# Group-norm statistics moved from VectorE's bn_stats to ScalarE's accumulator passes in a Mamba-then-attention kernel

## The chip, the cores and the metric

The kernel runs on one core of one Trainium2 chip. The metric is the device time of one execution in microseconds; the kernel before took 8108.69 us (median of three runs, 8093.1 to 8114.99). The engines are named as the profile names them: PE is TensorE's matmul, PEld its weight load, DVE is VectorE, ACT is ScalarE, POOL is GpSimd, SP issues DMAs. L464 is line 464 of the kernel before.

## The reference

The input x is 4 × 512 × 64 × 64 in float32: 4 batches, 512 channels, 4096 positions. Two blocks follow one another, each on a group norm of its input:

```python
x = x + mamba_block(gn(x))        # layer 0
x = x + linear_attention(gn(x))   # layer 1

def gn(v, G=32, eps=1e-5):        # mean and variance over 16 channels and all positions
    g = v.reshape(B, G, C // G, H, W)
    m, s = mean(g, (2, 3, 4)), var(g, (2, 3, 4))
    return ((g - m) / sqrt(s + eps)).reshape(v.shape)
```

The Mamba block normalises the channels of every position, splits the 512 channels into four chunks of 128, and runs a state-space scan over the 4096 positions of each chunk (256 inner channels, 16 states each), gated by a silu. Its output is normalised again, projected and added to x; the sum is called x1 here. The attention block needs the mean and the variance of x1 over a whole batch before it can start, because its group norm goes over all positions. These statistics of x1 are what the change is about.

## The kernel before, in words

Positions are cut into tiles of 512 (NT = 8 a batch), so a tile of x or x1 is 128 partitions × 4 channel groups × 512 (NC = 4). A *step* is one chunk of one tile of one batch: 4 × 8 × 4 = 128 steps in that order, and a step has 16 *slots* (SLOTS). "Tile (1,2)" is tile 2 of batch 1. In a slot, `slot` (L618) issues for two groups of 32 inner channels with 4 states: two scans on VectorE (L632), whose decay factors dA come from an exponential on ScalarE into one of three PSUM buffers (`decay`, L606, issued three scans ahead), whose inputs bx come from POOL (`drive`, L614, issued two slots ahead), and a product of the states with C on VectorE (L655), whose other factor c_all PE puts into a single PSUM buffer. PE then folds the states into y. In slots 4 and 11 of a step two products stand behind each other, in 5 and 12 none.

Everything else is woven in by hand: at the end of each slot, `after` (L1006) runs what is due and takes pieces from generators in the queues `ahead` (the norm of the next tile), `late` (a finished tile leaving), `rest` (attention of the batch before) and `light` (statistics of the next batch's input). The program order on each engine is the order in which this Python issues. Engines work in order, so an instruction on ScalarE stands behind all that was issued before it. Two spots of a step load ScalarE most: in slot 3 two softplus between two activation table loads (L1025, L512, L1027), in slot 10 a silu over 2048 elements between two loads (L946, L1047); the decays of the next slot come behind them.

A queue's piece says with what it yields when it may go on: a bare `yield` waits for the credit that limits matmul work per slot, `yield "free"` doesn't.

A finished tile leaves through `projected` (L433), four slots after the accumulating DMA of L461 has added x to the projection. Before, four `bn_stats` on VectorE (L464) then take the tile's statistics in two pieces of two, each 128 × 512, the tile is stored to x1 in DRAM by SP, and its SBUF buffer (one of three, shared with attention and the input statistics) is released two slots later. This takes place in the step of the next tile's last chunk, in most cases in slots 2 and 3. Behind the last tile of a batch, `attention` starts; `stats_end` (L313) turns the 8 × 6 numbers of each channel into a mean and a variance (four `bn_aggr`, L317) and then into the group's scale and offset. The attention of the last batch has no loop beside it and runs alone at the end of the kernel, and so do the last tile's statistics.

Of the kernel before, what the change touches and what calls it, by code (L numbers as in the profile page):

```python
# [8 lines left out]
F32 = mybir.dt.float32  # L9
BF16 = mybir.dt.bfloat16  # L10
AF = mybir.ActivationFunctionType
ALU = mybir.AluOpType
AX = mybir.AxisListType

P = 128
T = 512
# [8 lines left out]
def kernel(  # L25
# [24 lines left out]
    nc = tc.nc  # L50
    B, C, L = x.shape
    NC = C // P
    NT = L // T
# [11 lines left out]
    small = ctx.enter_context(tc.tile_pool(name="small", bufs=2))  # L65
    wk = ctx.enter_context(tc.tile_pool(name="wk", bufs=2))
# [12 lines left out]
    def work_bank(name, behind=1):  # L79
        held[0] += behind  # L80
        return ps_w.tile([P, T], F32, tag="w", name=name)

    def free(n=1):
        held[0] -= n

    def later(n, what):

        done = []

        def both():  # L90
            what()
            done.append(True)

        if now[0] is None:
            both()
        else:
            due.append((now[0] + n, both))
        return done
# [5 lines left out]
    def until(*done):  # L104
        while not all(done):
            yield "wait"

    def pause(n):
        return until(later(n, lambda: None))

    def room(when="wait"):

        while now[0] is not None and held[0] >= limit[0]:
            yield when
# [3 lines left out]
    def cols(v, b):  # L118
        return v[b].rearrange("(c p) l -> p c l", p=P)

    def mm(out_, lhsT, rhs, abreast=1, **how):

        work["mm"] += (0.25 if rhs.dtype == BF16 else 1.0) * rhs.shape[-1] / T / abreast
        nc.tensor.matmul(out_, lhsT, rhs, **how)  # L124
# [9 lines left out]
    def no_tile(spare=0):  # L134
        return now[0] is not None and held_x[0] + spare >= TILES

    def new_tile(name):
        held_x[0] += 1
        return wk.tile([P, NC, T], F32, tag="x", name=name, bufs=TILES)
# [168 lines left out]


    def stats_tile(name):  # L310
        return small.tile([P, NC, NT, 6], F32, tag="stats", name=name)

    def stats_end(stats, name):  # L313

        mv = small.tile([P, NC, 2], F32, tag="mv", name=f"mv_{name}")
        for c in range(NC):
            nc.vector.bn_aggr(mv[:, c, :], stats[:, c, :, :].rearrange("p t s -> p (t s)"))  # L317
        cm = small.tile([P, NC], F32, tag="cm", name=f"cm_{name}")
        nc.vector.tensor_copy(cm, mv[:, :, 0])
        yield from room()  # L320
        pm = work_bank(f"pm_{name}")
        mm(pm[:, 0:NC], grp, cm, start=True, stop=True)
        gm = small.tile([P, NC], F32, tag="gm", name=f"gm_{name}")
        nc.vector.tensor_copy(gm, pm[:, 0:NC])
        dev = small.tile([P, NC], F32, tag="dev", name=f"dev_{name}")
        nc.vector.tensor_tensor(dev, cm, gm, ALU.subtract)
        nc.vector.tensor_tensor(dev, dev, dev, ALU.mult)
        nc.vector.tensor_tensor(dev, dev, mv[:, :, 1], ALU.add)
        pv = pm[:, NC : 2 * NC]
        mm(pv, grp, dev, start=True, stop=True)  # L330
        gr = small.tile([P, NC], F32, tag="gr", name=f"gr_{name}", bufs=4)
        nc.vector.tensor_scalar(gr, pv, 1e-5, None, ALU.add)
        free()
        nc.gpsimd.tensor_tensor(gr, gr, mhalf, ALU.pow)
        off = small.tile([P, NC], F32, tag="off", name=f"off_{name}", bufs=4)
        ngm = small.tile([P, NC], F32, tag="ngm", name=f"ngm_{name}", bufs=4)
        nc.vector.tensor_scalar(ngm, gm, -1.0, None, ALU.mult)
        nc.vector.tensor_tensor(off, ngm, gr, ALU.mult)
        return gr, off, ngm
# [93 lines left out]
    def projected(ym, stats, x1, b, t):  # L433

        nm = f"{b}_{t}"
        yield from layer_norm(ym, f"b_{nm}", False)
        while no_tile():
            yield "wait"
        xt = new_tile(f"xr_{nm}")
        taken = []  # L440

        def take(o, pp):
            nc.scalar.activation(xt[:, o, :], pp, AF.Identity, bias=pb[:, o : o + 1])
            free()

        for o in range(NC):
            yield from room()
            pp = work_bank(f"pp_{nm}_{o}")
            for c in range(NC):
                mm(  # L450
                    pp, w_pr[:, c, o * P : (o + 1) * P], ym[:, c, :],
                    start=(c == 0), stop=(c == NC - 1),
                )
                if c == 1:
                    yield "more"
            taken.append(later(1, lambda o=o, pp=pp: take(o, pp)))
            yield
        yield from until(*taken)
        yield from pause(1)

        nc.gpsimd.dma_start(xt, cols(x, b)[:, :, t * T : (t + 1) * T], accum_op=ALU.add)  # L461
        yield from pause(4)
        for o in range(NC):
            nc.vector.bn_stats(stats[:, o, t, :], xt[:, o, :])  # L464
            if o % 2:
                yield
        nc.sync.dma_start(x1, xt)
        later(2, free_x)


    def inputs(f, xn, c, nm):
# [220 lines left out]
    def stats0(stats, b):  # L692

        for t in range(NT):
            xt = yield from load_x(b, t, "s")
            yield
            for c in range(NC):
                nc.vector.bn_stats(stats[:, c, t, :], xt[:, c, :])
                if c == NC - 1:
                    later(1, free_x)  # L700
                if c % 2:
                    yield "wait" if c == NC - 1 else None

    def attention(b, x1s, stats):
# [49 lines left out]

        fetch(0, "a")
        yield
        norm = yield from stats_end(stats, f"b{b}")
        yield
        for v in range(NT * SUB):
            t, u = divmod(v, SUB)  # L760
# [62 lines left out]
        gr, _, ngm = norm  # L823
# [46 lines left out]
        for o in range(NC):  # L870
            for k in range(P // BLK):
                r = slice(k * BLK, (k + 1) * BLK)
                v = m3[r, o, o * P + k * BLK : o * P + (k + 1) * BLK]
# [35 lines left out]
    norms, stats1, x1s = {}, {}, {}  # L909
# [6 lines left out]
    def input_norm(b):  # L916
        stats = stats_tile(f"st0_{b}")
        yield from stats0(stats, b)
        norms[b] = yield from stats_end(stats, f"a{b}")
        yield  # L920

    def tile_norm(b, t):
# [5 lines left out]

    def leave(b, t):
        if t == 0:  # L930
            stats1[b] = stats_tile(f"st1_{b}")
            x1s[b] = [
                dram.tile([P, NC, T], F32, tag="x1", name=f"x1_{b}_{i}", bufs=3 * NT)
                for i in range(NT)
            ]
        ym = xn[b, t][:, :, NTAP - 1 : NTAP - 1 + T]
        yield from projected(ym, stats1[b], x1s[b][t], b, t)
        if t == NT - 1:
            add_to(rest, attention(b, x1s[b], stats1[b]))
# [10 lines left out]
    def add_to(queue, pieces):  # L950
        queue.append([pieces, None])
# [3 lines left out]
    def one(queue, may=ANYWHERE):  # L955
# [10 lines left out]
        return False  # L966

    run(input_norm(0))
    run(tile_norm(0, 0))
    run(step_inputs(0))  # L970
# [21 lines left out]
    with tc.manual_schedule():  # L992
        credit, seen, mix, held[0], held_x[0] = 0.0, work["mm"], iter(()), 0, 0
        for n, (b, t, c) in enumerate(steps):
            f, nm = fs[n], names[n]
# [6 lines left out]
            if c == 0 and t == 0 and b + 1 < B:  # L1002
                add_to(light, input_norm(b + 1))
            assert c != 2 or not ahead
            for s in range(SLOTS):
                def after():  # L1006
# [21 lines left out]
                    if s == 6 and before is not None:  # L1028
                        pb_, pt_, pc_ = steps[n - 1]
                        with_skip(before, xn[pb_, pt_], pc_)  # L1030
                        if pc_ == NC - 1:
                            add_to(late, leave(pb_, pt_))
# [46 lines left out]
    out_proj(fs[N - 1], xn[B - 1, NT - 1], NC - 1, names[N - 1])  # L1079
    with_skip(fs[N - 1], xn[B - 1, NT - 1], NC - 1)  # L1080
    add_to(late, leave(B - 1, NT - 1))
    while late or rest:
        one(late) or one(rest)
# [53 lines left out]
```

## Time and profile before

| | us |
|---|---|
| median of three runs | 8108.69 |
| the profiled execution, device time | 8103.21 |
| its span, first to last instruction | 8101.5 |
| DVE busy | 7158.1 (88%) |
| POOL busy | 6888.6 (85%) |
| PE busy | 6487.2 (80%) |
| ACT busy | 5365.5 (66%) |
| L464, bn_stats of x1 on DVE, 128 of them | 80.6, mean 671 ns |
| L606, decays on ACT, 4096 | 2787.8, mean 689 ns |

A row of the groups gives the line, engine, operation, output and inputs with their shape, then after the first bar the busy time and the mean of one in ns, after the second the engine's idle time just before these instructions and what ended it. A row of the waits gives who waited for whom, the sum in us, how often, and the longest. A row of the timeline gives start and duration in us, the engine, line and operation, how many followed one another, and in brackets the idle time ahead of it and what ended that.

### The profile page before, as it was taken

What the parts mean: (1) busy time and instruction counts of PE and PEld (TensorE: products, weight loads), DVE (VectorE), ACT (ScalarE), POOL (GpSimd) and SP (SyncE); (2) the same over time, 40 slices, a digit from 0 to 9 for tenths busy, and PEclk for the clock granted to TensorE, in tenths of its full rate; (3) what the DMA queues carried; (4) which work ended last, traced back from release to release, by engine and by line L of the source; (5) the groups of instructions that cost most, each with busy time, mean ns of one, the idle gap of its engine ahead of it and who ended that gap; (6) DMA issues with size and microseconds to landing.
All of it is one profiled execution on the core that took longest, in us unless ns stands there. A gap on an engine that the chain in (4) does not pass through costs nothing.

```text
span 8101.5 us, 92105 instructions
## 1 busy us (share of the span) xinstructions
PE 6487.2 (80%) x24800; PEld 2116.5 (26%) x24800; DVE 7158.1 (88%) x6891; ACT 5365.5 (66%) x7841; POOL 6888.6 (85%) x4597
## 2 busy tenths in 40 slices
PE   5677777667888888887788888888788888888699
PEld 1111112111222222322132222222122222322144
DVE  5999999999999999999999999999999999999700
ACT  4666677676677767676777767676777777766421
POOL 4999999999999988899989989898999989889600
PEclk8787878788899999998898999899799999999699
DMA  5666666666666666676756666677666666677402
GB/s 159 167 164 159 154 147 153 157 155 166 162 169 156 156 161 153 173 191 169 170 144 171 165 163 159 149 182 184 157 163 157 154 154 148 157 185 187 113 32 88
DMA packets 829195, 1265.95 MB, mean 156 GB/s; under 512 B 183912, under 2 KB 317560, under 8 KB 816384
## 3 DMA queue, kind: packets, MB, share of 16 engines
q1 hardware_dynamic: 804736, 1222.32, 60.1%
q0 software_dynamic: 16896, 33.56, 2.4%
q10 hardware_dynamic: 7040, 4.20, 0.2%
q8 instruction: 194, 3.18, 0.2%
q14 instruction: 329, 2.70, 0.1%
HBM read 1052.78 MB, written 206.57 MB: 155 GB/s over the span
## 4 chain that ended last, share of the span: by engine, by line
DVE 21%; PE 19%; DMA 19%; POOL 15%; issue 10%; SPq 9%; ACT 6%; POOLq 0%; DVEq 0%; ACTq 0%
DVE h L632 13%; POOL bx L614 11%; DMA d_all<-d_rows 11%; DVE h L655 6%; SPq L581 6%; PE pq L124 5%; DMA b_all<-b_rows 4%; SPq L531 3%; ACT dA L606 3%; PE pc L124 3%; PE pr L124 3%; PE y L124 2%; DMA c_sb<-c_rows 2%; POOL h L643 2%; POOL dt L520 1%
## 5 line engine op out<-in xcount | busy, mean ns | idle before, releaser
L614 POOL TENSOR_TENSOR bx<-d_all,b_all 128x1024 f32<-128x1024 f32 x2048 | 4815.8, 2370 | 51.4 <-DVE h L632 34.1
L632 DVE TENSOR_TENSOR_SCAN h<-dA,st,bx 128x512 f32<-128x512 f32 x3584 | 4425.2, 1268 | 59.0 <-ACT dA L606 49.5
L606 ACT ACTIVATE dA<-d_all,a_t 128x512 f32<-128x512 f32 x4096 | 2787.8, 689 | 1936.0 <-DVE h L632 1893.6
L655 DVE TENSOR_TENSOR h<-h,c_all 128x768 f32<-128x768 f32 x2048 | 1908.8, 932 | 301.9 <-PE c_all L124 293.5
L643 POOL TENSOR_TENSOR h<-h,c_sb 128x512 f32<-128x512 f32 x1024 | 1298.6, 1268 | 145.8 <-DMA c_sb<-c_rows 49.7
L124 PE MATMUL y<-h,fold 128*32 128x512 f32 x8192 | 1287.8, 705 | 140.7 <-POOL h L643 136.9
L124 PE MATMUL c_all<-parts,sel 128*128 128x384 bf16 x1024 | 369.8, 361 | 1112.7 <-DVE h L655 1110.5
L124 PE MATMUL pc<-xn,w_cv 128*128 128x512 f32 x2048 | 1068.2, 657 | 189.4 <-DVE xn L406 127.2
L124 PE MATMUL pq<-w_qk,xa 128*128 128x512 f32 x2048 | 989.8, 616 | 1.6 <-ACT xa L344 1.6
L632 DVE TENSOR_TENSOR_SCAN h<-dA,bx 128x512 f32<-128x512 f32 x512 | 601.6, 1207 | 60.3 <-ACT dA L606 55.9
L124 PEld LDWEIGHTS pc<-xn,w_cv 128*128 128x128 f32 x2048 | 394.1, 203 | 819.3 <-issue 455.9
L124 PEld LDWEIGHTS <-sel 128*128 128x128 bf16 x1280 | 127.5, 100 | 1792.5 <-DVE h L655 1552.8
L642 POOL COPY st<-h 128x4 f32<-128x4 f32 x1024 | 207.3, 202 | 436.4 <-DVE h L632 392.9
L124 PEld LDWEIGHTS pq<-w_qk,xa 128*128 128x128 f32 x2048 | 404.2, 200 | 455.6 <-issue 432.3
L124 PE MATMUL pr<-xb,m 128*128 128x512 f32 x1024 | 503.8, 630 | 7.3 <-DMA xb<-x 4.0
L124 PE MATMUL pp<-xn,w_pr 128*128 128x512 f32 x1024 | 487.5, 602 | 3.8 <-DVE xn L406 3.8
L124 PEld LDWEIGHTS y<-h,fold 128*32 128x32 f32 x8192 | 171.0, 115 | 719.2 <-issue 291.0
L124 PE MATMUL y<-xz,dg 32*32 32x512 f32 x2048 | 340.5, 741 | 0.0
L679 POOL TENSOR_TENSOR xz<-xz 128x512 f32<-128x512 f32 x256 | 325.0, 1270 | 2.7 <-ACT xz L676 2.7
L124 PE MATMUL pd<-xz,w_xp 128*128 128x512 f32 x512 | 317.3, 752 | 7.8 <-ACT xz L946 7.8
L520 POOL TENSOR_TENSOR dt<-dt,xz 128x1024 f32<-128x1024 f32 x128 | 302.1, 2360 | 22.1 <-DMA c_rows<-dt 20.9
L730 ACT ACTIVATE kq<-pq 128x512 f32<-128x512 f32 x256 | 150.9, 590 | 242.9 <-PE pq L124 240.0
(156 smaller groups left out, 5919.5 us busy)
## 6 DMA issues: line engine op xcount, KB each, us to landing
d_all<-d_rows SPq DMA_DIRECT2D x2048, 256.0 KB, 6.6
b_all<-b_rows SPq DMA_DIRECT2D x4096, 64.0 KB, 2.2
d_rows<-dt SPq DMA_DIRECT2D x256, 512.0 KB, 3.7
c_sb<-c_rows SPq DMA_DIRECT2D x4096, 16.0 KB, 1.8
xs<-in_x_dram SPq DMA_DIRECT2D x32, 1024.0 KB, 6.5
xn<-in_x_dram SPq DMA_DIRECT2D x32, 1024.0 KB, 5.8
xr<-in_x_dram POOLq DMA_DIRECT2D x32, 1024.0 KB, 10.6
x<-xr SPq DMA_DIRECT2D x32, 1024.0 KB, 6.6
```

The source lines that it names most:

```text
L124: nc.tensor.matmul(out_, lhsT, rhs, **how)
L520: nc.gpsimd.tensor_tensor(f["both"][:, 1], f["both"][:, 0], f["xz"][:, 0], ALU.mult)
L531: nc.sync.dma_start(d[k * BLK : (k + 1) * BLK, v], src)
L581: nc.sync.dma_start(dst[k * BLK : (k + 1) * BLK, :], rows_[q * KS + k, :].partition_broadcast(BLK))
L606: nc.scalar.activation(dAs[k], fs[n]["d_all", e][:, 0, j, :], AF.Exp, scale=a_t[:, e, j, q : q + 1])
L614: nc.gpsimd.tensor_tensor(bxs[g], fs[n]["d_all", e][:, 1, jj * 2 : jj * 2 + 2, :], bc(b_all[g // JJ], 2), ALU.mult)
L632: nc.vector.tensor_tensor_scan(h[:, j, :], dAs.pop(2 * g + i), bxs[g][:, i, :], 0.0 if t == 0 else st[:, c, e, q, j : j + 1], ALU.mult, AL ...
L642: nc.gpsimd.tensor_copy(st[:, c, e, q, :], h[:, :, T - 1])
L643: nc.gpsimd.tensor_tensor(h[:, :, CUT:], h[:, :, CUT:], bc(c_sb.pop(g // JJ), NJ), ALU.mult)
L655: nc.vector.tensor_tensor(own, own, bc(c_all[g // JJ], 2), ALU.mult)
L679: nc.gpsimd.tensor_tensor(f["xz"][:, 1, e, :], f["xz"][:, 1, e, :], f["xz"][:, 0, e, :], ALU.mult)
L730: nc.scalar.activation(qk[i], pq, AF.Relu)
```

## The change

For the first tile of a batch the four `bn_stats` stay; their result is aggregated at once, into a mean and a variance per channel. For the other seven tiles, ScalarE runs two passes over each of the four 128 × 512 parts of the tile: `Identity` with the negated mean of the first tile as its bias, and `Square` with the same bias. Each writes a throwaway output (in the buffers called "res") and has its row sum put out by the accumulator, into `sum` and `square`. The passes come in pairs, one pair per piece, and the pieces yield "free": a tile takes four slots instead of two, independent of the credit. At the end of the batch, `shifted_end` adds up the sums over the tiles and makes mean and variance of them. The statistics of the kernel's input (`stats0`) stay on `bn_stats`.

```diff
     def stats_tile(name):
-        return small.tile([P, NC, NT, 6], F32, tag="stats", name=name)
-
-    def stats_end(stats, name):
-        mv = small.tile([P, NC, 2], F32, tag="mv", name=f"mv_{name}")
+        return small.tile([P, NC, NT, 6], F32, tag="stats", name=name, bufs=1)
+
+    def aggregate(stats, name):
+        mv = small.tile([P, NC, 2], F32, tag="mv", name=f"mv_{name}", bufs=4)
         for c in range(NC):
             nc.vector.bn_aggr(mv[:, c, :], stats[:, c, :, :].rearrange("p t s -> p (t s)"))
+        return mv
+
+    def stats_end(mv, name):
         cm = small.tile([P, NC], F32, tag="cm", name=f"cm_{name}")
...
         nc.gpsimd.dma_start(xt, cols(x, b)[:, :, t * T : (t + 1) * T], accum_op=ALU.add)
         yield from pause(4)
-        for o in range(NC):
-            nc.vector.bn_stats(stats[:, o, t, :], xt[:, o, :])
-            if o % 2:
-                yield
+        yield from shifted(stats, xt, t, nm)
         nc.sync.dma_start(x1, xt)
         later(2, free_x)
+
+    def shifted_stats(b):
+        f = {"first": small.tile([P, NC, 1, 6], F32, tag="first", name=f"first_{b}")}
+        for v in ("sum", "square"):
+            f[v] = small.tile([P, NC, NT], F32, tag=v, name=f"{v}_{b}")
+        return f
+
+    def shifted(f, xt, t, nm):
+        if t == 0:
+            for o in range(NC):
+                nc.vector.bn_stats(f["first"][:, o, 0, :], xt[:, o, :])
+                if o % 2:
+                    yield
+            f["mv"] = aggregate(f["first"], f"first_{nm}")
+            f["off"] = small.tile([P, NC], F32, tag="moff", name=f"moff_{nm}")
+            nc.vector.tensor_scalar(f["off"], f["mv"][:, :, 0], -1.0, None, ALU.mult)
+            nc.vector.memset(f["sum"][:, :, 0:1], 0.0)
+            nc.vector.tensor_scalar(f["square"][:, :, 0], f["mv"][:, :, 1], float(T), None, ALU.mult)
+            return
+        for o in range(NC):
+            for v, func in (("sum", AF.Identity), ("square", AF.Square)):
+                unused = wk.tile([P, T], F32, tag="res", name=f"{v}_{nm}_{o}", bufs=2)
+                nc.scalar.activation(
+                    unused, xt[:, o, :], func, bias=f["off"][:, o : o + 1],
+                    accum_out=f[v][:, o, t : t + 1],
+                )
+            yield "free"
+
+    def shifted_end(f, name):
+        mv = small.tile([P, NC, 2], F32, tag="mv", name=f"mv_{name}", bufs=4)
+        for v in range(2):
+            nc.vector.tensor_reduce(mv[:, :, v], f[("sum", "square")[v]], AX.X, ALU.add)
+        nc.vector.tensor_scalar(mv, mv, 1.0 / L, None, ALU.mult)
+        d2 = small.tile([P, NC], F32, tag="d2", name=f"d2_{name}")
+        nc.vector.tensor_tensor(d2, mv[:, :, 0], mv[:, :, 0], ALU.mult)
+        nc.vector.tensor_tensor(mv[:, :, 1], mv[:, :, 1], d2, ALU.subtract)
+        nc.vector.tensor_tensor(mv[:, :, 0], mv[:, :, 0], f["mv"][:, :, 0], ALU.add)
+        return mv
...
-        norm = yield from stats_end(stats, f"b{b}")
+        norm = yield from stats_end(shifted_end(stats, f"b{b}"), f"b{b}")
...
-        norms[b] = yield from stats_end(stats, f"a{b}")
+        norms[b] = yield from stats_end(aggregate(stats, f"a{b}"), f"a{b}")
...
-            stats1[b] = stats_tile(f"st1_{b}")
+            stats1[b] = shifted_stats(b)
```

## The prediction

> **What bounds the kernel now.** I read the busy shares first, then the groups of instructions by form, then the waits of VectorE, and last the timeline of single stretches. Shares and groups:
>
> ```profile
> PE 6487.2 (80%) x24800; PEld 2116.5 (26%) x24800; DVE 7158.1 (88%) x6891; ACT 5365.5 (66%) x7841; POOL 6888.6 (85%) x4597
> ...
> L632 DVE TENSOR_TENSOR_SCAN h<-dA,st,bx 128x512 f32<-128x512 f32 x3584 | 4425.2, 1268 | 59.0 <-ACT dA L606 49.5 <-POOL bx L614 8.5
> ...
> L464 DVE BATCH_NORM_STATS2 st<-xr 128x6 f32<-128x512 f32 x128 | 80.6, 671 | 29.3 <-DMA xr<-in_x_dram 29.3
> ```
>
> The loop of 2048 slots runs from 119 us to 7631 us of the span, 3.67 us a slot; behind it the last tile and the last attention take another 470 us. A slot without extras lasts 3.21 us, which is exactly VectorE's two scans (L632) and one product (L655), back to back. VectorE sets the pace, POOL (L614, 2370 ns a slot) is close behind it. L464, the line that the change removes for seven tiles of eight, costs 80.6 us in all. VectorE's own waits, longest first:
>
> ```profile
> DVE h L655 <- PE c_all L124: 293.5, 172, 5.7
> DVE kq L737 <- PE pk L124: 241.0, 40, 7.6
> DVE h L632 <- ACT dA L606: 105.4, 54, 46.2
> ```
>
> The second lies in the tail. The first and third say where VectorE already waits in the loop, and there time taken off VectorE comes back as waiting. So the timeline matters. ScalarE in slots 2 to 6 of the step in which tile (0,4) leaves (batch 0, tile 4):
>
> ```profile
> 1430.55 0.69 ACT L606 ACTIVATE dA<-d_all,a_t 128x512 f32<-128x512 f32 x1 [1.35 <-DVE h L632]
> 1432.91 0.69 ACT L606 ACTIVATE dA<-d_all,a_t 128x512 f32<-128x512 f32 x1 [1.67 <-DVE h L632]
> 1434.95 0.69 ACT L606 ACTIVATE dA<-d_all,a_t 128x512 f32<-128x512 f32 x1 [1.35 <-DVE h L632]
> 1435.66 1.28 ACT L1025 ACT_TABLE_LOAD   x1
> 1436.96 1.26 ACT L512 ACTIVATE dt<-pt,dtb 128x512 f32<-128x512 f32 x2
> 1438.24 1.28 ACT L1027 ACT_TABLE_LOAD   x1
> 1439.54 1.30 ACT L606 ACTIVATE dA<-d_all,a_t 128x512 f32<-128x512 f32 x2
> ```
>
> ScalarE idles 1.35 to 1.67 us ahead of a decay (dA) in most slots, waiting for a scan to free a PSUM buffer. In slot 3 it doesn't: two table loads and two softplus run 3.86 us without a gap. The decay at 1439.54 ends at 1440.23, and its scan starts at 1441.49 (timeline of VectorE): 1.26 us to spare. VectorE meanwhile:
>
> ```profile
> 1430.44 1.26 DVE L464 BATCH_NORM_STATS2 st<-xr 128x6 f32<-128x512 f32 x2
> 1431.61 1.27 DVE L632 TENSOR_TENSOR_SCAN h<-dA,st,bx 128x512 f32<-128x512 f32 x1
> ...
> 1465.32 1.28 DVE L632 TENSOR_TENSOR_SCAN h<-dA,st,bx 128x512 f32<-128x512 f32 x1 [1.11 <-ACT dA L606]
> ```
>
> A pair of statistics takes 1431.61 − 1430.44 = 1.17 us of VectorE, a tile's two pairs 2.35. The last row is slot 12 of that step: ScalarE's silu between two loads (L946, L1047) makes the decay late, and there is no slack left.
>
> **What the skill says.** The Trainium skill, "ScalarE: Activation LUTs", What ACT_TABLE_LOAD costs: a pointer operand adds 93 ns, back-to-back instructions overlap by 93 ns, and one with a pointer bias takes 280 ns + 0.833 ns an element, here 707 ns. The trace agrees: Square without a pointer 615 ns, L344 with two pointers 804 ns, loads 1283 ns. The same page, What it computes, says that an ACTIVATE can give an accumulator output; I found no price for it there, and no row of before shows one. "SBUF — State Buffer", Who interferes with whom: a VectorE instruction with one SBUF input doesn't contend with GpSimd, one with two does. L464 indeed stays within 657 to 695 ns; L338 (two inputs) averages 1766 ns, but 0.16 us in the tail, where POOL is idle.
>
> **The change, part by part.**
>
> *Removed:* 28 × 4 bn_stats; 27 tiles × 2.35 = 63.5 us in the loop, 2.47 us in the tail. *Added:* 28 × 8 ScalarE passes. Two passes back to back take 2 × (707 − 93) = 1.23 us without the accumulator. The accumulator's price is bounded below by nothing, above by some 0.38 us each, two of the 186 ns fixed parts that the page gives an ACTIVATE; I take one, 0.19. A pair is then 1.6 us (1.23 to 2.0). Both functions already run under the loaded tables, so no load is added. In the built order each pair stands behind slot work of ScalarE, one pair per slot over four slots, and the decays of the next slot are queued behind it.
>
> *Tiles with pairs in slots 2 to 5, nothing else there* ((0,3) to (0,6), (2,7)). The load moves 1.17 us earlier, since one bn pair ahead of it is gone; the decay behind it gets 1.6 us of statistics in front; its scan moves 2.35 us earlier. Slack 1.26 + 1.17 − 1.6 − 2.35 = −1.52: a stall. Gain 2.35 − 1.52 = 0.83 a tile, ×5 = 4.2 us. The pairs in slots 2, 4 and 5 are covered by the 1.35 us gaps and the three decays ahead.
>
> *The same slots, but with input statistics (L698) in slot 3* ((0,1), (0,2), (0,7), (1,7)): that work leaves 2.4 us of slack instead of 1.26, so the stall is 0.4. But bx (L614) ends only 0.4 to 1.5 us ahead of its scan later in these steps, and POOL doesn't start earlier: 1.2 a tile, 4.8 us.
>
> *Tiles at a slot 4 where c_all is late* ((1,1), (2,1), (3,2), (3,4); waits of 1.1 to 4.0 us). At 6638.81 PE's pc waits for softplus, then pq and c_all follow, so this chain starts with the load. It moves 1.17 us earlier, less some 0.2 for the first pair: 1.0 a tile, 4.0 us. *Four tiles starting in slot 3* ((1,4), (2,4), (3,1), (3,3)): their first bn pair already lies under such a wait of 2.28 us, the second doesn't: 1.1 a tile, 4.4 us.
>
> *Nine tiles whose pairs run into the silu* ((1,2), (1,3), (2,2), (2,3) in slots 7 to 10; (1,5), (1,6), (2,5), (2,6), (3,5) in 8 to 11). The pair behind slot 10 adds its 1.6 us to the wait without slack at slot 12, and the earlier pairs, one a slot beside the takes of pc, y and pz (0.6 us each), pile up some 0.9: −2.5 against +2.35, a loss of 0.15, 1.3 us in all. In (1,6) and (2,6) VectorE also waited 1.2 to 1.3 us for the tile's DMA, which is no longer late: +2.5. *Tile (3,6)* meets neither softplus nor silu: +2.4.
>
> Together 4.2 + 4.8 + 4.0 + 4.4 − 1.3 + 2.5 + 2.4 = 21.0 us off the loop.
>
> *Paid back on VectorE.* First tile of a batch: four bn_aggr (0.25 us each) and three small instructions (0.2), 1.6 × 4 = 6.4, with waits for POOL's port 7 (up to 20). Its bn_stats stay. End of a batch: six instructions at 0.2 for four bn_aggr (1.05), in the loop 1 (up to 15 with the port). *In the tail* nothing hides it: eight passes at 0.80 = 6.5 for 2.47, and 0.2: 4.2 us. Sum 12.2.
>
> *Moved for nothing:* the x1 store leaves SP two slots later, past some ten other issues, and its tile is freed two slots later. Attention on batches 0 and 1 therefore fetches later and ends its first phase 18 slots later, still well inside the loop; its reader of the last x1 tile is later still. The accumulators' throwaway outputs share the two "res" buffers with attention's stores; a store is 2.3 us in flight and two slots (6.4 us) old when the pass comes. The reshuffling moves PE's waits by perhaps ±10 us; I count 0.
>
> Net 21.0 − 12.2 = 8.8 us faster. Against the profiled execution, 8103.2, that is 8094.4; its median stands 5.5 higher at 8108.7, so I forecast 8100.
>
> **Rivals.** *The saving arrives* (A): ScalarE is only 66% busy, and if its pairs slip into gaps everywhere, 63.5 − 12.2 = 51 us: 8057. For it: the 1.35 us gaps. Against: slots 3 and 12. *ScalarE becomes the bound* (B, slower): with a pair of 2.4 us, slots 4 to 6 no longer hold decays and pair. Then the first five tiles lose 0.7 each, four gain nothing, the next eight break even, nine lose 2.5 at the silu (23), the tail costs 7.5, VectorE's small work 8, less what (3,6) saves: some 40 us, 8150. It decides from a pair of about 2.2 us on, or if late takes on ScalarE hold PE's three work banks. *Everything freed is waited for elsewhere* (C), POOL or c_all, and only the costs stay: +12, 8121.
>
> **How the numbers follow.** Forecast 0.46, A 0.21, B 0.16, C 0.17. With pairs of 1.23 us my sum gives −25 us, with 2.0 about +8, so the forecast's own range is 8080 to 8115. A measurement here can't tell less than 0.3% (24 us) from no change: A is faster, with some of the cheap-pair end (0.23 together), B slower (0.17), the rest 0.60. The range takes in C and most of the way to A and B: 8060 to 8132.
>
> **What would show it.** After, the bn_stats of x1 are 16 instructions (some 11 us) on VectorE and ScalarE gains about 224 passes of 0.7 to 0.9 us, some 180 us busy. VectorE's wait for dA should grow from 105 to some 135 us: about 1.5 in slot 5 of the plain tiles, about 3.6 in slot 12 of the silu tiles. The tail should be 4 us longer. I am wrong if passes last over 1.1 us, if waits for c_all grow by tens of us in batches 1 and 2, or if slot 12 keeps 1.1.

## The result, and the profile after

The changed kernel takes 8085.74 us (median of 13 runs, 8080.2 to 8092.56) against 8100.28 us for the kernel before on the same chip (13 runs, 8093.1 to 8114.99). The ratio is 0.998, with a 95% interval of 0.9971 to 0.9988: a gain of 10 to 23 us that can be told from nothing, but stays inside the 0.3% that the prediction called no change. The profiled execution took 8087.92 us (before 8103.21), its span 8086.2 us (before 8101.5).

The share of each engine, VectorE's scans with the x1 statistics that remain (first the page's row, then one from the groups by form), and ScalarE's new groups by form. Columns: busy us and mean ns of one, then the idle time ahead.

```profile
PE 6471.4 (80%) x24800; PEld 2115.5 (26%) x24800; DVE 7113.0 (88%) x6815; ACT 5514.5 (68%) x8289; POOL 6890.3 (85%) x4597
...
L673 DVE TENSOR_TENSOR_SCAN h<-dA,st,bx 128x512 f32<-128x512 f32 x3584 | 4420.5, 1267 | 80.6 <-ACT dA L647 75.4
...
L482 DVE BATCH_NORM_STATS2 first<-xr 128x6 f32<-128x512 f32 x16 | 10.1, 671 | 0.0
```

```profile
L494 ACT ACTIVATE sum<-xr,moff 128x512 f32<-128x512 f32 x112 | 80.2, 716 | 9.8 <-DMA xr<-in_x_dram 9.3
L494 ACT ACTIVATE square<-xr,moff 128x512 f32<-128x512 f32 x112 | 79.6, 711 | 0.7
...
L494 ACT ACTIVATION_READ_ACCUMULATOR sum<-xr,moff 128x1 f32 x112 | 21.1, 189 | 0.0
L494 ACT ACTIVATION_READ_ACCUMULATOR square<-xr,moff 128x1 f32 x112 | 21.0, 188 | 0.0
```

Each accumulator costs an instruction of its own, 188 ns. In the timeline further down consecutive instructions overlap, and a pair of passes occupies ScalarE for 1.43 us (from 1433.13 to the decay at 1434.56), not the sum of its records, 1.8. VectorE's waits:

```profile
DVE h L696 <- PE c_all L124: 298.2, 165, 6.0
DVE kq L778 <- PE pk L124: 242.4, 42, 7.6
DVE h L673 <- ACT dA L647: 130.1, 64, 46.7
DVE mv_b L503 <- ACT sum L494: 32.0, 1, 32.0
```

The wait for decays grew by 25 us (from 105.4). The last row stands in the tail, in place of the 26.8 us that L464 waited there for the last tile's DMA. The loop and the tail of both kernels, before first, in the view of stretches (span, then busy time of PE, weight loads, VectorE, ScalarE and POOL):

```profile
118.70:7630.70 7512.00, 6000.72 (x23179) 1894.85 (x23179) 7092.49 (x6730) 5235.16 (x7647) 6875.63 (x4578) 0.89 0.66 162
7630.70:8101.50 470.80, 435.23 (x1508) 199.17 (x1508) 28.85 (x77) 97.06 (x150) 5.07 (x5) 0.92 0.18 58
```

```profile
120.30:7611.80 7491.50, 5983.84 (x23179) 1894.06 (x23179) 7049.84 (x6656) 5378.42 (x8079) 6874.63 (x4576) 0.89 0.66 163
7611.80:8086.20 474.40, 435.61 (x1508) 199.20 (x1508) 26.35 (x75) 102.80 (x166) 5.59 (x6) 0.92 0.17 58
```

VectorE works 42.6 us less in the loop and the loop is 20.5 us shorter; the other 22 us became waiting. The tail is 3.6 us longer and the loop starts 1.6 us later, which gives the 15.3 us of the two profiled executions. The loop's start differs by some 5 us among all the traces here, so those 1.6 us are not the change's.

In the step in which tile (0,4) leaves, from slot 3 on, ScalarE does this:

```profile
1425.33 0.69 ACT L647 ACTIVATE dA<-d_all,a_t 128x512 f32<-128x512 f32 x1 [1.35 <-DVE h L673]
1426.05 0.72 ACT L494 ACTIVATE sum<-xr,moff 128x512 f32<-128x512 f32 x1
1426.68 0.19 ACT L494 ACTIVATION_READ_ACCUMULATOR sum<-xr,moff 128x1 f32 x1
1426.77 0.71 ACT L494 ACTIVATE square<-xr,moff 128x512 f32<-128x512 f32 x1
...
1429.25 1.28 ACT L1066 ACT_TABLE_LOAD   x1
1430.55 1.27 ACT L553 ACTIVATE dt<-pt,dtb 128x512 f32<-128x512 f32 x2
1431.84 1.28 ACT L1068 ACT_TABLE_LOAD   x1
1433.13 0.72 ACT L494 ACTIVATE sum<-xr,moff 128x512 f32<-128x512 f32 x1
1433.76 0.19 ACT L494 ACTIVATION_READ_ACCUMULATOR sum<-xr,moff 128x1 f32 x1
1433.85 0.71 ACT L494 ACTIVATE square<-xr,moff 128x512 f32<-128x512 f32 x1
1434.46 0.19 ACT L494 ACTIVATION_READ_ACCUMULATOR square<-xr,moff 128x1 f32 x1
1434.56 1.28 ACT L647 ACTIVATE dA<-d_all,a_t 128x512 f32<-128x512 f32 x2
```

The first pair (1426.05) hides in the gap behind a decay. The next one stands between the softplus's second load and the decays, with ScalarE busy without a gap since 1428.55, and VectorE meets it:

```profile
1435.26 2.46 DVE L673 TENSOR_TENSOR_SCAN h<-dA,st,bx 128x512 f32<-128x512 f32 x2 [0.88 <-ACT dA L647]
```

At the silu the wait is longer. Slot 12 of the step in which tile (1,5) leaves:

```profile
3574.63 1.28 DVE L673 TENSOR_TENSOR_SCAN h<-dA,st,bx 128x512 f32<-128x512 f32 x1 [3.18 <-ACT dA L647]
```

### The profile page after: what moved, and what is told of

Its sections match the earlier page's. It is cut to its first block, busy times and chain, and to the rows that moved or that the text cites. A ratio compares the mean times of both kernels' runs of the same rounds, so it can differ in the third digit from the quotient of the medians.

```text
span 8086.2 us, 92449 instructions
## 1 busy us (share of the span) xinstructions
PE 6471.4 (80%) x24800; PEld 2115.5 (26%) x24800; DVE 7113.0 (88%) x6815; ACT 5514.5 (68%) x8289; POOL 6890.3 (85%) x4597
## 4 chain that ended last, share of the span: by engine, by line
DVE 22%; PE 19%; DMA 17%; POOL 14%; issue 10%; ACT 9%; SPq 8%; POOLq 0%; DVEq 0%; ACTq 0%
DVE h L673 14%; POOL bx L655 10%; DMA d_all<-d_rows 9%; DVE h L696 7%; PE pq L124 5%; SPq L622 5%; DMA b_all<-b_rows 4%; ACT dA L647 3%; PE pc L124 3%; PE pr L124 3%; SPq L572 3%; PE y L124 3%; POOL h L684 2%; PE pp L124 1%; DMA c_sb<-c_rows 1%
## 5 line engine op out<-in xcount | busy, mean ns | idle before, releaser
L124 PE MATMUL pr<-xb,m 128*128 128x512 f32 x1024 | 500.4, 626 | 24.8 <-DMA xb<-x 16.5
```

## The experiments

The steps in which tiles leave (the fourth of each tile's four steps) are compared one by one between traces, by the starts of the scans. Each ratio is to runs of the kernel before on the same chip, whose medians were 8094.7 to 8102.4 us. "First tiles" are the four steps in which tile 0 of a batch leaves. Differences of the whole loop between single profiles are not read below some 8 us: one experiment below has the median of the kernel before and a loop 7.7 us longer in its profile.

**The passes left out.** The sums stay at zero, so the x1 statistics of seven tiles of eight are not computed.

```diff
-            nc.vector.memset(f["sum"][:, :, 0:1], 0.0)
+            nc.vector.memset(f["sum"], 0.0)
+            nc.vector.memset(f["square"], 0.0)
...
-            for v, func in (("sum", AF.Identity), ("square", AF.Square)):
-                unused = wk.tile([P, T], F32, tag="res", name=f"{v}_{nm}_{o}", bufs=2)
-                nc.scalar.activation(
-                    unused, xt[:, o, :], func, bias=f["off"][:, o : o + 1],
-                    accum_out=f[v][:, o, t : t + 1],
-                )
             yield "free"
```

> The kernel after without its ScalarE passes: seven of eight tiles have no statistics at all (sum and square stay at zero but for the first tile's part), the four slots of waiting stay. It shows what taking bn_stats off VectorE is worth when nothing is put on ScalarE. My theory (the pairs behind softplus and silu are what eats the saving): the nine silu tiles gain their full 2.35 us, which is about 1.9 more than now (17 us), the five plain ones some 0.3 each more until POOL's bx is the next bound, the tail loses its eight passes (6 us): about 25 us less than the kernel after, 8061 us. The rival that POOL and PE's c_all eat the saving whatever ScalarE does: only the tail's 6 us, 8080 us, and slot 12 stays longer than 3.6 us in the silu tiles.

8056.48 us, ratio 0.9946 (0.9933 to 0.9958). The total is not the test that it was meant to be: without the passes the last attention no longer waits for its last tile, and the tail shrinks to 448.9 us, 25 less than in the changed kernel, which the passes could never give. In the loop the theory holds for the nine silu steps, which together are 16.5 us shorter than in the changed kernel. But the loop as a whole is 7489.1 us, only 2.4 less. What was freed came back in other places: the two steps of (1,1) and (2,1) are 2.8 us longer each, the first tiles 1.5, and the steps in which nothing leaves 9.5; waits for c_all and bx grew by some 15 us in all. For the same loss in the same two steps the cause is shown below, in the kernel without the shift; the 9.5 us were not traced step by step.

**Each pass twice.** A pair is then some 2.8 us.

```diff
-            for v, func in (("sum", AF.Identity), ("square", AF.Square)):
+            for v, func in 2 * (("sum", AF.Identity), ("square", AF.Square)):
```

> The kernel after with each pass issued twice (the second writes the same sums), so a pair costs about 2.8 us of ScalarE in place of the measured 1.41; VectorE's work is unchanged. My theory: every added microsecond of a pair stands in the chain at slots 3 and 10, so slot 5 of plain tiles stalls 1.4 us longer, slot 12 of silu tiles by up to 4 (their pairs pile up), the tail grows by 5.6 us: about 70 us more than the kernel after, some 8155 us, slower than the kernel before. The rival (ScalarE is 68% busy and has room): only the tail's 5.6 us, 8092 us.

8174.94 us, ratio 1.0094 (1.008 to 1.0107), 20 us above my 8155 and far from the rival's 8092. Against before four of the five plain steps are 3.0 us longer and the fifth 3.6, four of the silu steps 3.5 to 4.6, the other five 5.9, and VectorE's wait for dA rises to 234.2 us in all. This is the prediction's rival B, met on the way from 1.4 to 2.8 us a pair: the first 1.4 us cost the loop hardly anything (2.4 us, less than I read from single profiles), the second 1.4 us cost it 87. Where between the two it begins was not measured.

**No pair in the slots with softplus and silu.**

```diff
         for o in range(NC):
+            while now[0] is not None and now[0] % SLOTS in (3, 8, 9, 10):
+                yield "free"
             for v, func in (("sum", AF.Identity), ("square", AF.Square)):
```

> The kernel after, but no pair is issued in slots 3, 8, 9 and 10; it waits for the next slot. My theory: slot 5 of the plain tiles loses its stall of 1.0 us, though POOL's bx allows only some 0.3 to 0.5 of it, and slot 12 of the nine silu tiles loses its added 1.45 to 2.1 us, 15 us in all: 8070 us. The rival (what is left of the saving is lost to reshuffled attention and to POOL, wherever the pairs stand): 8086 us, within 4.

8091.25 us, ratio 0.9986 (0.998 to 0.9993): no better than the changed kernel (0.998). The mechanism worked where it was aimed: the wait for dA fell from 130.1 to 108.3 us, and the nine silu steps became 13.9 us shorter. It did not arrive: the leaving steps of (1,1), (2,1) and (3,4) gave 2.1, 2.0 and 8.3 us back, the steps in which nothing leaves 3.8. My expectation of 8070 failed; the rival's 8086, given within 4, was missed by 5, but it is the nearer of the two. Why these steps grew was not traced.

**Only the pacing.** The kernel before, with one bn_stats a slot, independent of the credit, as the passes are issued, instead of two in a slot.

```diff
             nc.vector.bn_stats(stats[:, o, t, :], xt[:, o, :])
-            if o % 2:
-                yield
+            yield "free"
```

> The kernel before with the pacing of the change alone: bn_stats stays on VectorE, but one instruction per slot over four slots, independent of the credit, so the tile is stored and freed two slots later and attention is reshuffled as in the kernel after. My theory: the pacing is worth nothing by itself, 8100 us within 6. The rival (the pacing, not the engine, brought the gain): 8086 us.

8099.19 us, ratio 0.9999 (0.999 to 1.0007). The spreading over four slots, which also delays the x1 store and attention's fetches, is worth nothing by itself in the total. It does move single steps by up to 10 us, which matters when the steps of the prediction are judged below.

**The first tile's small instructions.** Two of them moved to ScalarE in the changed kernel:

```diff
-            nc.vector.tensor_scalar(f["off"], f["mv"][:, :, 0], -1.0, None, ALU.mult)
+            nc.scalar.activation(f["off"], f["mv"][:, :, 0], AF.Copy, scale=-1.0)
...
-            nc.vector.tensor_scalar(f["square"][:, :, 0], f["mv"][:, :, 1], float(T), None, ALU.mult)
+            nc.scalar.activation(f["square"][:, :, 0], f["mv"][:, :, 1], AF.Copy, scale=float(T))
```

> The changed kernel with the first tile's two scalings (the negated mean, the variance times 512) on ScalarE instead of VectorE; nothing else. Theory S: the first tiles lose 9.8 us in all because their small VectorE instructions wait beside POOL (the negation alone took 6.3 us for four); with two of them gone the four steps lose about 3 instead of 9.8, the loop falls by 6 to some 7485, the time is some 8080. Rival: those steps lose because the work behind them is reordered; then they keep +9.8, and the time stays at 8086.

and all of them added to the kernel before:

```diff
+        if t == 0:
...
+            for o in range(NC):
+                nc.vector.bn_aggr(mv[:, o, :], stats[:, o, 0, :])
...
+            nc.vector.tensor_scalar(off, mv[:, :, 0], -1.0, None, ALU.mult)
+            nc.vector.memset(square[:, :, 1:2], 0.0)
+            nc.vector.tensor_scalar(square[:, :, 0], mv[:, :, 1], float(T), None, ALU.mult)
         nc.sync.dma_start(x1, xt)
```

> The kernel before, with only the first tile's added VectorE instructions (four aggregations of six numbers, two scalings, one memset) behind its statistics, their results unused. Theory S: the four steps in which a first tile leaves become some 2.3 us longer each, 9 in all, and the time some 8109. Rival (these instructions cost 1.6 us a batch, as forecast, or hide in waits): +6 or less, 8100 to 8106, and the steps grow by 1.6 or less each.

Without the two, 8078.52 us, ratio 0.9976 (0.9965 to 0.9986), 7 us under the changed kernel; the intervals overlap, but the steps are plain: the first tiles lose 2.3 us instead of 9.8. With all of them in the kernel before, 8105.14 us, ratio 1.0009 (1.0001 to 1.0017), inside the rival's range and 4 us under theory S. The four steps are 1.4 to 2.5 us longer each and 7.7 in all, halfway between S (9) and the most that the rival allows (6.4); two of the four are above its bound of 1.6. So this run alone does not decide, but it shows that these instructions cost more than time of their own; with the other run, where taking two of them off VectorE removed 7.5 of the 9.8 us, the first tiles' loss is mainly these instructions. The changed kernel's timeline shows why, on VectorE and then on POOL:

```profile
525.15 0.37 DVE L317 BATCH_NORM_AGGREGATE mv_first<-first 128x2 f32<-128x6 f32 x4
525.56 2.14 DVE L487 TENSOR_SCALAR moff<-mv_first 128x4 f32<-128x4 f32 x1
527.63 0.16 DVE L489 TENSOR_SCALAR square<-mv_first 128x4 f32<-128x4 f32 x1
527.64 0.06 DVE L488 MEMSET sum<- 128x4 f32 x1
```

```profile
525.33 2.35 POOL L655 TENSOR_TENSOR bx<-d_all,b_all 128x1024 f32<-128x1024 f32 x1
```

The four aggregations run freely beside POOL. The negation of four elements begins just after POOL's bx and ends with it (527.70 and 527.68); its twin, which comes behind it, takes 0.16 us. In all four batches the negation ends within 0.03 us of the POOL instruction beside it, and lasts 1.0 to 2.14 us. The Trainium skill, "SBUF — State Buffer", Who interferes with whom, frees a VectorE instruction with one SBUF input only outside what it calls the 2-port modes, and names `tensor_scalar`, which the negation is, among those that can enter them and then block. The waiting fits that; no run tells which mode it was in.

**No first tile at all.** All eight tiles by passes, without a bias; no aggregation, no scalings, no bn_stats of x1.

```diff
-        if t == 0:
-            ...
-            return
         for o in range(NC):
...
-                    unused, xt[:, o, :], func, bias=f["off"][:, o : o + 1],
+                    unused, xt[:, o, :], func,
...
-        nc.vector.tensor_tensor(mv[:, :, 0], mv[:, :, 0], f["mv"][:, :, 0], ALU.add)
```

> All eight tiles by ScalarE passes, without the first tile's mean: no statistics of x1 on VectorE, no aggregation and scaling behind the first tile, no pointer bias in the passes. Theory S: the four first tiles' loss (9.8) and their statistics (9.4 on VectorE) go, their own passes cost some 5, and shorter pairs save some 3 at the silu: some 17 us off, 8069; the four steps turn from +9.8 to about -5. Rival F (what is taken off VectorE from here on is waited for at c_all and bx, as when the passes were cleared out of the way of the decays): at most 4 us off, 8082 to 8086, with c_all and bx waits 10 us higher.

8070.99 us, ratio 0.9965 (0.9953 to 0.9978), theory S within 2 us in the total, and right in the first tiles (+9.8 became −5.2). The passes take 0.62 us instead of 0.71: the pointer bias costs the 93 ns that the prediction cited, within 2 ns (716 and 711 against 625 and 618 ns). It is the simplest version and 15 us faster than the changed kernel; that the sums are then taken about zero costs precision where means are large against deviations, and no run here varies the inputs.

**One pass instead of two.** As the last, with the sum as an accumulator output of the instruction that takes the projection from PSUM, and the input's mean added at the end.

```diff
-            nc.scalar.activation(xt[:, o, :], pp, AF.Identity, bias=pb[:, o : o + 1])
+            nc.scalar.activation(
+                xt[:, o, :], pp, AF.Identity, bias=pb[:, o : o + 1],
+                accum_out=stats["sum"][:, o, t : t + 1],
+            )
...
-            for v, func in (("sum", AF.Identity), ("square", AF.Square)):
+            for v, func in (("square", AF.Square),):
...
+        nc.vector.tensor_tensor(mv[:, :, 0], mv[:, :, 0], f["mv"][:, :, 0], ALU.add)
```

> As the kernel without the shift, and the sum pass gone too: the sum of the projection is an accumulator output of the instruction that takes it from PSUM, and the input's mean, known from the first normalisation, is added at the end. ScalarE then spends one pass of 0.62 us a column instead of two. Theory S: as without the shift, less some 3 us in the tail and some 8 at the silu: 8058. Rival F: the loop stays within 5 us of the changed kernel's 7491, only the tail's 3 us come off: 8080. A longer take (0.19 us for reading the accumulator, with PE's banks held longer) could take 5 us back.

8068.36 us, ratio 0.996 (0.9947 to 0.9972). Neither number held: theory S said 8058, rival F 8080 with a loop near 7491. What F says holds for this step alone: with half the passes gone the loop is 7478.0 us against 7476.5 with both, so nothing of what was taken off ScalarE arrived that single profiles can tell. It is the fastest version that computes everything, level with the one before it within what the runs tell.

**Where freed time goes: TensorE's clock.** Without the shift, the steps of (1,1) and (2,1) lose 2.7 and 2.8 us against the changed kernel, as they did without the passes. (In these rows a float32 matmul counts twice: the filler below issues nine and leaves 18 records, so "x4" is two matmuls of the program.) TensorE in the step of (1,1), the changed kernel first, then the one without the shift; in brackets the idle time ahead:

```profile
2577.51 0.69 PE L124 MATMUL pk<-kq 128*64 128x64 f32 x16
2578.73 1.99 PE L124 MATMUL pc<-xn,w_cv 128*128 128x512 f32 x4 [0.53 <-DVE kq L778]
2580.55 0.38 PE L124 MATMUL pq<-bqk,sel 128*128 128x512 bf16 x1
2580.76 1.88 PE L124 MATMUL pq<-w_qk,xa 128*128 128x512 f32 x4
2582.48 0.33 PE L124 MATMUL c_all<-parts,sel 128*128 128x384 bf16 x1
```

```profile
2568.53 0.69 PE L124 MATMUL pk<-kq 128*64 128x64 f32 x16
2571.89 3.34 PE L124 MATMUL pc<-xn,w_cv 128*128 128x512 f32 x4 [2.67 <-ACT dt L541]
2575.03 0.63 PE L124 MATMUL pq<-bqk,sel 128*128 128x512 bf16 x1
2575.46 2.04 PE L124 MATMUL pq<-w_qk,xa 128*128 128x512 f32 x4
2577.34 0.33 PE L124 MATMUL c_all<-parts,sel 128*128 128x384 bf16 x1
```

In the changed kernel pc waits for VectorE's use of pk (L778), in the other for softplus (L541), 2.1 us longer, and the same four records then take 3.34 us instead of 1.99. The Trainium skill, "TensorE: Matmul & The Clock Gate", What's actually happening, gives the array half its clock after an idle window of about 3.4 us, and says that these windows run freely. The traces record the clock that was granted, 1.0 or 0.5 of full speed, and the stretches of each are multiples of 3.41 us (the last is cut off by the end), which agrees. But less idle than a whole window is enough here. The groups of four pc records in ten traces (all here but the two below), by TensorE's idle time ahead of them:

| idle ahead, us | groups of four pc | mean us of a group | over 2.3 us | mean granted clock in the group |
|---|---|---|---|---|
| under 0.1 | 1839 | 1.96 | 3% | 0.99 |
| 0.1 to 1.0 | 326 | 2.42 | 28% | 0.87 |
| 1.0 to 1.8 | 319 | 2.58 | 40% | 0.82 |
| 1.8 to 2.4 | 98 | 2.84 | 68% | 0.73 |
| 2.4 to 3.2 | 146 | 3.07 | 92% | 0.65 |
| over 3.2 | 122 | 3.44 | 100% | 0.57 |

Clock and duration go together without an exception: the 2251 groups at full clock took 1.99 us or less, the 599 at less than full clock all took over 2.3 us.

To see whether the idle is the cause, it was filled, in the two steps alone, with matmuls into the unused half of pk's bank, which nobody reads. The filler stands behind every pk that these steps issue, which is three times each; the one in slot 3 stands ahead of pc.

```diff
-            pk = work_bank(f"pk_{b}_{v}")[:, 0 : C // 2].rearrange("p (c d) -> p c d", c=NC)
+            bank = work_bank(f"pk_{b}_{v}")
+            pk = bank[:, 0 : C // 2].rearrange("p (c d) -> p c d", c=NC)
...
+            if now[0] is not None and now[0] // SLOTS in (43, 75):
+                for i in range(9):
+                    nc.tensor.matmul(
+                        bank[:, C // 2 : C], w_qk[:, 0, 0:P], w_qk[:, 0, 0 : C // 2],
+                        start=True, stop=True,
+                    )
```

> The kernel without the shift, with nine extra matmuls of 256 columns (about 1.9 us, into the unused half of pk's bank, read by nobody) behind pk in steps 43 and 75 alone, where TensorE idles 2.67 and 2.24 us ahead of pc and then runs pc's four and pq's four matmuls in 3.34 + 2.47 and 2.49 + 3.33 us instead of the 1.99 + 2.10 they take in the changed kernel after 0.53 us of idle. Theory W (the idle costs the clock): with the gap filled pc and pq take about 2.0 and 2.1 us again although pc starts no earlier, c_all comes some 1.7 us sooner, and each of the two steps is 1.5 to 1.8 us shorter; the whole time moves by less than the runs can tell, about 3 us. Rival V (operands or banks slow them): pc and pq keep 5.8 us in all, and the steps keep or lengthen their time.

pc and pq took 1.88 and 2.09 us in both steps, as theory W said. The steps did not get shorter (+0.3 and +0.1 us): the nine matmuls took 4.15 us, twice what I had reckoned, and VectorE waited for pk's bank until they had ended. The total was 8071.81 us (0.9972, 0.9961 to 0.9984). So again with four (`range(4)`):

> As the kernel with the gap filled, with four of the extra matmuls instead of nine: each had run as two, so that nine took 4.08 us, outlasted the gap and held up VectorE, which waited for pk's bank to be finished (3.9 to 4.4 us in slot 3). Four should take 1.8 us, and VectorE's addition of pk wait that long. Theory W: pc and pq take 2.0 and 2.1 us again, start no later than before, c_all comes 1.7 us sooner and finds VectorE 1.7 us later: its wait of 3.6 us all but goes, and steps 43 and 75 become about 1.7 us shorter than without the filling, instead of the 0.3 and 0.1 longer that they became with nine. Rival V (the clock matters, but the step is set otherwise): the steps keep their time within 0.5 us. The total shows nothing of it (3 us).

The step of (1,1) on TensorE:

```profile
2568.91 0.69 PE L124 MATMUL pk<-kq 128*64 128x64 f32 x16
2569.53 1.99 PE L785 MATMUL pk<-w_qk 128*128 128x256 f32 x8
2572.03 1.99 PE L124 MATMUL pc<-xn,w_cv 128*128 128x512 f32 x4 [0.50 <-ACT dt L541]
2573.85 0.38 PE L124 MATMUL pq<-bqk,sel 128*128 128x512 bf16 x1
2574.06 1.88 PE L124 MATMUL pq<-w_qk,xa 128*128 128x512 f32 x4
2575.78 0.33 PE L124 MATMUL c_all<-parts,sel 128*128 128x384 bf16 x1
```

pc waits for softplus as before, runs in 1.99 us, and c_all is on time. The granted clock over the four pc records is the first number behind POOL's in these rows; the changed kernel, then the one without the shift, then the one with the gap filled:

```profile
2578.73:2580.72 1.99, 1.99 (x5) 0.94 (x6) 1.99 (x3) 1.98 (x3) 1.91 (x3) 1.00 1.09 218
2571.89:2575.23 3.34, 3.34 (x5) 1.31 (x6) 2.21 (x3) 3.31 (x7) 3.34 (x3) 0.57 0.94 186
2572.03:2574.02 1.99, 1.99 (x5) 0.94 (x6) 1.99 (x3) 1.96 (x3) 1.99 (x2) 1.00 1.02 194
```

The two steps are 2.03 and 1.98 us shorter than without the filling, where I had expected 1.7. In slots 3 and 4, where pc and c_all stand, it is 1.3 and 1.2 us: 3.5 and 3.1 us off slot 4, less some 2 us that VectorE waits for the filler in slot 3. The other 0.7 and 0.8 us come in slot 15, behind the filler of slot 11; in the step of (1,1) that one cut a gap of 3.27 us ahead of c_all to 1.43, and the fold matmuls behind took 1.06 us at full clock instead of 1.94 at half. The idle was the cause. The total, 8074.46 us (0.9967, 0.9955 to 0.9979), shows nothing of 4 us, as said.

## Why the prediction was right, and where its steps were not

The time lies in the range and in the case that I held likeliest, no change within 0.3%. Part of the agreement is cancelling: my own sum said 8.8 us faster, the profiled executions say 15.3. The 5.5 us that I added for the median of before came from three runs; over 13 runs that median is 8100.3, below the profiled execution, not above it.

| step of the sum, us | forecast | measured | pacing alone |
|---|---|---|---|
| plain tiles (5) | −4.2 | −2.2 | +2.2 |
| input statistics in slot 3 (4) | −4.8 | −8.5 | −5.1 |
| late c_all in slot 4 (4) | −4.0 | −10.3 | +4.5 |
| start in slot 3 (4) | −4.4 | −8.8 | −5.6 |
| silu tiles (9), DMA gain included | −1.2 | −2.2 | −1.4 |
| tile (3,6) | −2.4 | −1.4 | −2.2 |
| first tiles | +7 | +9.8 | +0.8 |
| other steps (end of batch, reshuffling) | +1 | +3.1 | +14.6 |
| tail | +4.2 | +3.6 | −0.6 |
| start of the loop | 0 | +1.6 | +2.1 |

The last column is the experiment that left bn_stats on VectorE, likewise against the profile of before. Its profile is the slowest of its 13 runs, so its sum (+9 us) says little; single groups say more. Where this column is far from zero, an agreement of forecast and measurement proves little.

*Right.* The bound is VectorE, and what is taken off it returns mostly as waiting where ScalarE has no slack: of 42.6 us, 22. The pass has the price I took: 0.71 us and 0.19 for the accumulator. That they overlap brings the pair to 1.43 instead of 1.6 us, the cheap side of my value. Four plain tiles gained 0.7 to 1.0 us, forecast 0.83, and the pacing alone leaves these four within 0.2 us. At the silu, slot 12 took 2.1 us more in the five steps whose pairs stand in slots 8 to 11 and 1.2 to 1.5 in the other four (forecast 2.5), and the nine tiles come out near zero, as reckoned. ScalarE's busy time grew by 149 us, forecast some 180. The wait for dA went to 130.1 us, forecast 135. The tail is 3.6 us longer, forecast 4.2.

*Mis-sized, and the largest.* The term is "It moves 1.17 us earlier, less some 0.2 for the first pair: 1.0 a tile" for the four tiles at a late c_all: measured 2.5 to 2.65 each. I had let the chain from softplus to c_all move as a block. In the step of (3,2), before and then after:

```profile
6638.81 3.42 PE L124 MATMUL pc<-xn,w_cv 128*128 128x512 f32 x4 [2.65 <-ACT dt L512]
```

```profile
6618.96 1.99 PE L124 MATMUL pc<-xn,w_cv 128*128 128x512 f32 x4 [1.46 <-ACT dt L553]
```

pc starts 1.2 us earlier in this step, and 1.0 us earlier in that of (3,4), which is the block that I had reckoned. But its four records also went from 3.42 and 3.39 us to 1.99, at a granted clock of 0.57 and 0.56 before and 1.00 after: the larger part of the gain is TensorE's clock, which the sum had not. Idle of 1.46 and 1.58 us does not always keep the clock (40% of the table's row are slow), so that it did in both steps is in part luck. In (1,1) and (2,1) the kernel before had run pc at full clock after 2.90 us of idle, two of the few that do; in the changed kernel pc waits for VectorE instead of softplus and c_all comes in time. What the filling experiments show there is the other side: where pc waits for softplus again, the clock takes the whole gain away. A duration read off a row of before was taken for a property of the instruction, where it was one of the idle time before it.

*Mis-sized.* The first tiles: four aggregations at 0.25 us and three small instructions at 0.2, 7 us for four batches with the port, measured 9.8, of which two instructions carry 7.5. I had called on the skill for one input against two and left out its condition, the 2-port modes, and so priced the negation as nearly free of POOL; it is not.

*Right in sign for another reason.* The four tiles that start in slot 3 gained 8.8 us for 4.4, but 7.35 of it stand in (1,4) and (2,4), and there the pacing alone gains 3.71 and 3.69 us, with every bn_stats still on VectorE. It moves pieces of attention between slots: two steps ahead some 5 to 6.5 us are gained, in the step behind 10 to 11 are lost, in both runs alike. My "I count 0" for the reshuffling holds for the sum and not for single steps, and most of this group's gain is luck; the other two tiles gave 0.25 and 1.2 us for 1.1 each. The same run shows where (2,7) comes from, +1.45 us where I expected −0.83: the pacing alone makes it +1.97. In (0,7) and (1,7) the pacing alone gains 1.9 and 3.2 us, so that only (0,1) and (0,2) test the term for input statistics. They gained 2.2 and 3.3 us for 1.2 each: slot 5 grew by 0.2 and 0.0 us where I had put 1.15 for stall and bx. The further 0.9 us of (0,2) were not traced.

*Wrong, without weight.* The DMA gain of 2.5 us in (1,6) and (2,6) did not come: these two steps lost 0.75 us each, where the other silu tiles of their group gained 0.15. In (1,6) the DMA's 1.22 us and the pair behind it stood in slot 4, which lasts 6.86 us before and after: VectorE now waits 2.69 us for c_all there instead of 0.16.

*The rivals.* B is real, but not at the price of this pair: at 2.8 us a pair the kernel is 0.94% slower, at 1.43 it is not. A could not have come at any price of the pass, since with the first tile's work kept and no pass at all the loop is only 22.9 us shorter than before. C was put too bluntly, but where the giving back was traced it is of C's kind: with less on ScalarE, TensorE idles at other places, and waits for c_all take back what the decays no longer need. My list of terms gave most of its words to the passes; they cost the loop hardly anything, and treating the first tile apart cost 15 us.

## What to carry to other kernels

When work is moved from the bounding engine to one with gaps, what has to be costed is the handful of places without slack and the new small instructions, not the moved work: here 224 passes cost the loop hardly anything, and 28 tiny instructions with 16 statistics cost it 15 us. Small VectorE instructions beside a busy POOL are worth timing one by one: here a four-element negation took nearly as long as POOL's instruction, and moving it to ScalarE helped. A TensorE duration next to an idle gap is not a constant: read the granted clock and the idle ahead of it in both traces before moving it as a block. And when a change also moves other work to other slots, a run with that movement alone tells which steps are the change's own.

## What the runs showed that I had not expected

- A matmul group after 2.4 to 3.2 us of idle took 3.07 us on average instead of 1.96; all 599 slow groups ran below the full granted clock. Filling a gap of 2.2 to 2.7 us with matmuls that nobody reads made slots 3 and 4 of a step 1.2 to 1.3 us shorter, and a second gap the step's end 0.7 to 0.8.
- A VectorE instruction with a single SBUF input of four elements lasted 2.14 us beside POOL against 0.16 us behind it, while aggregations of six elements next to it took 0.15 us each on average.
- Reading ScalarE's accumulator is an instruction of 188 ns of its own; between two passes only about half of it shows.
